# L2 attention of a four-layer net: the place of the weighing in each unit's order, and one reciprocal for two query tiles

## The chip, the cores and the metric

The kernel runs on one core of a Trainium2 chip. The metric is the device time of one execution in microseconds. Five engines work beside each other, each through its own instructions in order: TensorE (PE, its weight loads shown apart as PEld), VectorE (DVE), ScalarE (ACT), GpSimd (POOL) and SyncE (SP). They wait for each other by semaphores.

## The reference

Tokens `x` have the shape (8, 512, 128): 8 batches of 512 tokens. Four layers follow each other, each a half feed-forward, an attention and a half feed-forward. The change lies in the attention of layer 2:

```
def _L2_attn_ref(x, Wq, Wk, Wv, Wo, bo):        # 16 heads (H) of 64 (DH)
    q, k, v = x @ Wq, x @ Wk, x @ Wv            # each split into heads
    scores = einsum('bihd,bjhd->bhij', q, k) * 64**-0.5 + slope * (i - j)
    scores = where(i >= j, scores, -1e30)       # causal
    attn = softmax(scores)
    out = einsum('bhij,bjhd->bihd', attn, v)
    return out @ Wo + bo
...
x = x + 0.5 * _L1_ffn_ref(_layernorm(x), ...)   # splines chosen by two argmaxes
x = x + 0.5 * _L2_ffn_ref(_layernorm(x), ...)   # one 128x128 matrix
x = x + _L2_attn_ref(_layernorm(x), ...)
x = x + 0.5 * _L2_ffn_ref(_layernorm(x), ...)
x = x + 0.5 * _L3_ffn_ref(_layernorm(x), ...)   # 8 experts, two chosen
```

## The kernel before

`l2_block` works through 64 units. A unit is one batch and one pair of heads (`jj` 0 and 1), so eight units make a batch. The 512 queries of a unit are four tiles (`i` 0 to 3) of 128 rows; because of the causal mask tile `i` needs only 128(i+1) keys.

The work on unit n is spread over several turns of one loop, so that different units overlap. The loop runs over n from -4 to 67. Its turn n holds, in this order on TensorE:

- three groups of four transposes of unit n-1's probabilities (`turn` with m = 4, 0, 1; `tp` L1732), each copied to SBUF by ScalarE (`pt` L1734);
- the projection of q and k for unit n+1 (`pp` L1674; ScalarE copies them, `qk` L1676);
- the scores of unit n for tiles 2 and 1 (`score`, `s` L1706). VectorE adds the bias, masks and takes the minimum in one instruction for each head (`e`, `m` L1710), and ScalarE takes the exponential and at the same time its row sum into `sums` (`e` L1713);
- the last two groups of transposes of unit n-1 (m = 2, 3);
- `norm(n, 3, 0)`: VectorE turns the row sums of tile 3 into reciprocals (`rc` L1740) and multiplies both heads' probabilities with them (`e` L1743), and then the same for tile 0;
- `works(3n)`: steps of other stages that are due here;
- half of the values of a pair of units (`vp` L1687; VectorE copies them, `v` L1688), and after a batch's last unit `leave` (`op` L1766), the output projection of that batch;
- `weigh(n - 2)`: the probabilities of unit n-2 times its values, sixteen matmuls of 128x64 weights (`o` L1757), copied by ScalarE (`att` L1760);
- `norm(n, 2, 1)` on VectorE;
- `works(3n + 1)`, more steps of other stages;
- the scores of unit n+1 for tiles 3 and 0, and `works(3n + 2)`.

The other stages' steps stand in a table `todo` under due places: for each batch the layer 1 feed-forward (`sp` L1048, `pa` L1138, VectorE lines L1054 to L1155, ScalarE's Gelu L1055 and tanh L1063), the two layer 2 feed-forwards (`op` L348, L351) and the layer 3 feed-forward (`lp` L366, `lm` L416 and `lg` L417 on VectorE; `yp` L384 with four VectorE instructions each, L386), with normalising and transposing between them (POOL L219 to L275, `pt` L314, copied at L321). A batch's steps come at the same places of each batch, so most stretches of eight units look alike.

The order on TensorE, ScalarE and VectorE is that of the recording (`tc.manual_schedule`). All TensorE results but the scores go through four PSUM banks (`bank`, tag "mm", 4 buffers): a new result waits until the last result in its bank has been read. The scores have two buffers of two banks each. The framework chooses which free bank a result gets.

```
def bank(name, shape=(P, 512)):
    return ps.tile(list(shape), F32, tag="mm", name=name, bufs=4)
...
with tc.manual_schedule(engines={mybir.EngineType.PE, mybir.EngineType.Activation, mybir.EngineType.DVE}):
    for n in range(-4, last + 4):
...
def works(at):
    for work in todo.pop(at, ()):
        work()
```

Of the kernel before, what the change touches and what calls it, by code (L numbers as in the profile page):

```python
# [8 lines left out]
F32 = mybir.dt.float32  # L9
I32 = mybir.dt.int32  # L10
AF = mybir.ActivationFunctionType
ALU = mybir.AluOpType
# [4 lines left out]
P = 128  # L17
# [127 lines left out]
class Net:  # L145
# [1496 lines left out]
    def l2_block(self, w1, w2, w3, xt0):  # L1642
# [9 lines left out]

        nc, tc, a = self.nc, self.tc, self.a
        wq, wo = self.wq, self.wo
        OFF = (0, 128, 384, 768)
        with ExitStack() as c:
            pool = c.enter_context(tc.tile_pool(name="a2", bufs=1))
            wk = c.enter_context(tc.tile_pool(name="a2w", bufs=2))
            ps = c.enter_context(tc.tile_pool(name="a2p", bufs=1, space=PSUM))

            bias = pool.tile([P, 16, 512], F32, tag="bias", name="bias")

            def bank(name, shape=(P, 512)):
                return ps.tile(list(shape), F32, tag="mm", name=name, bufs=4)

            qs, ks, vs, es, mins, sums, turned, atts = {}, {}, {}, {}, {}, {}, {}, {}

            def project(n):

                b, at = n // 8, n % 8 * P  # L1670
                outs = []
                for made, m in ((qs, 0), (ks, 1)):
                    pp = bank("pp")
                    nc.tensor.matmul(pp, lhsT=wq[:, m, at : at + P], rhs=xts[b], start=True, stop=True)  # L1674
                    t = made[n] = wk.tile([P, 512], F32, tag=f"qk{m}", name="qk")
                    outs.append(lambda t=t, pp=pp, m=m: nc.scalar.activation(t, pp, AF.Copy, scale=1.0 if m else -0.125))  # L1676
                return outs

            def values(n, half):

                b, at = n // 8, n % 8 * P
                if not half:
                    vs[n] = vs[n + 1] = wk.tile([P, 4, 2 * P], F32, tag="v", name="v", bufs=2)
                vp = bank("vp", (P, 2, 2 * P))
                for i in range(2):
                    s0 = (2 * half + i) * P
                    nc.tensor.matmul(vp[:, i, :], lhsT=xts[b][:, s0 : s0 + P], rhs=wq[:, 2, at : at + 2 * P], start=True, stop=True)  # L1687
                nc.vector.tensor_copy(vs[n][:, 2 * half : 2 * half + 2, :], vp)  # L1688
# [7 lines left out]
            def score(n, i):  # L1696

                if n not in es:
                    es[n] = wk.tile([P, 2, 1280], F32, tag="e", name="e")
                    mins[n] = wk.tile([P, 2, 4], F32, tag="m", name="m")  # L1700
                    sums[n] = wk.tile([P, 2, 4], F32, tag="sm", name="sm", bufs=3)
                w = P * (i + 1)
                s = ps.tile([P, 2, 512], F32, tag="s", name="s", bufs=2)
                for jj in range(2):
                    cut = slice(64 * jj, 64 * jj + 64)
                    nc.tensor.matmul(s[:, jj, 0:w], lhsT=qs[n][cut, i * P : (i + 1) * P], rhs=ks[n][cut, 0:w], start=True, stop=True)  # L1706
                outs = []
                for jj in range(2):
                    e = es[n][:, jj, OFF[i] : OFF[i] + w]
                    nc.vector.tensor_tensor_reduce(  # L1710
                        out=e, in0=s[:, jj, 0:w], in1=bias[:, n % 8 * 2 + jj, 512 - w : 512], scale=1.0, scalar=BIG,
                        op0=ALU.add, op1=ALU.min, accum_out=mins[n][:, jj, i : i + 1])
                    outs.append(lambda e=e, jj=jj: nc.scalar.activation(  # L1713
                        e, e, AF.Exp, bias=mins[n][:, jj, i : i + 1], scale=-1.0, accum_out=sums[n][:, jj, i : i + 1]))
                return outs

            def block(n, jj, i, kt):
                lo = OFF[i] + kt * P
                return es[n][:, jj, lo : lo + P]

            def turn(n, m):


                if m == 4:
                    blocks = [(jj, i, 2) for jj in range(2) for i in (2, 3)]
                else:
                    blocks = [(m // 2, i, 1) for i in (1, 2, 3)] + [(m // 2, 3, 3)] if m % 2 else [(m // 2, i, 0) for i in range(4)]
                if n not in turned:
                    turned[n] = wk.tile([P, 5, 512], F32, tag="pt", name="pt")
                tp = bank("tp", (P, 4, P))  # L1730
                for k, (jj, i, kt) in enumerate(blocks):
                    nc.tensor.transpose(tp[:, k, :], block(n, jj, i, kt), self.ident)  # L1732
                to = turned[n][:, m, :].rearrange("p (k q) -> p k q", q=P)
                return lambda: nc.scalar.copy(to, tp)  # L1734

            def norm(n, *tiles):

                for i in tiles:
                    rc = wk.tile([P, 2], F32, tag="rc", name="rc", bufs=4)
                    nc.vector.reciprocal(rc, sums[n][:, :, i])  # L1740
                    for jj in range(2):
                        e = es[n][:, jj, OFF[i] : OFF[i] + P * (i + 1)]
                        nc.vector.tensor_scalar(e, e, rc[:, jj : jj + 1], None, ALU.mult)  # L1743

            def weigh(n):
                b, p, t = n // 8, n % 8, turned.pop(n)
                if p == 0:
                    atts[b] = wk.tile([P, 8, 512], F32, tag="att", name="att", bufs=1)
                o = bank("o")
                for kt in range(4):  # L1750
                    for jj in range(2):
                        if kt == 2:
                            src = t[:, 4, 256 * jj : 256 * jj + 256]
                        else:
                            src = t[:, 2 * jj + kt % 2, 384:512] if kt == 3 else t[:, 2 * jj + kt, 0 : 512 - kt * P]
                        lo = (n % 2) * P + 64 * jj
                        nc.tensor.matmul(  # L1757
                            o[64 * jj : 64 * jj + 64, kt * P : 512], lhsT=vs[n][:, kt, lo : lo + 64], rhs=src,
                            start=(kt == 0), stop=(kt == 3), skip_group_check=True)
                nc.scalar.copy(atts[b][:, p, :], o)  # L1760
# [17 lines left out]
            n = 3 * (last - 5)  # L1778
# [3 lines left out]
            for b in range(NB):  # L1782
                n = 3 * (8 * b - 6)
# [12 lines left out]
                n = 3 * (8 * b + 11)  # L1796
# [3 lines left out]
# [4 lines that stand above are left out]
            def run(*outs):  # L1804
                for out in outs:
                    out()

            late = []
            with tc.manual_schedule(engines={mybir.EngineType.PE, mybir.EngineType.Activation, mybir.EngineType.DVE}):
                for n in range(-4, last + 4):  # L1810
                    here, prev, two = 0 <= n < last, 1 <= n <= last, 2 <= n <= last + 1
                    if n == -1:
                        run(*project(0))
                    outs, qk, exps = [], [], []
                    if prev:
                        outs = [turn(n - 1, m) for m in (4, 0, 1)]
                    if 0 <= n and n + 1 < last:
                        qk = project(n + 1)
                    if here:
                        exps = score(n, 2) + score(n, 1)  # L1820
                    run(*outs[:2], *late[:2], *outs[2:], *late[2:], *qk, *exps[:2])
                    late = []
                    if prev:
                        run(*[turn(n - 1, m) for m in (2, 3)])
                    run(*exps[2:])
                    if here:
                        norm(n, 3, 0)
                    works(3 * n)
                    if here:
                        values(n - n % 2, n % 2)  # L1830
                    if n >= 3 and (n - 3) % 8 == 7 and n - 3 < last:
                        leave((n - 3) // 8)
                    if two:
                        weigh(n - 2)
                    if here:
                        norm(n, 2, 1)
                    works(3 * n + 1)
                    if -1 <= n and n + 1 < last:
                        late = score(n + 1, 3)
                        late += score(n + 1, 0)  # L1840
                    if -3 <= n < 5:
                        slopes(n + 3)
                    works(3 * n + 2)
                assert not todo
# [198 lines left out]
```

## Time and profile before

| what | value |
|---|---|
| median of three executions | 2611.81 us (2608.92 to 2611.95) |
| profiled execution: its own time | 2632.98 us |
| profiled execution: span from first to last instruction | 2631.2 us |
| the L2 attention's stretch (1030 to 1876 us of the span) | 846 us |
| in it TensorE busy, VectorE busy, ScalarE busy | 809.1, 666.3, 587.3 us |
| granted TensorE clock in it | 1.00 |
| VectorE reciprocals at L1740 in the whole span | 256, of 159 ns in the middle |
| time of eight units in a steady batch (1353 to 1464, for example) | 111 us |

Times in the profile are microseconds from the start of the span. A timeline row has the start, the duration, the engine, line and operation, what it writes and reads, how many instructions it merges, and in brackets how long the engine had been idle before it and who ended that wait. A matmul's end is modelled: matmuls are pipelined, and a row can start a little before the one ahead of it ends. So the cost of a group of matmuls is best read from its start to the start of the next group.

### The profile page before, as it was taken

The page shows a single profiled execution, that of the slowest core. Times are in us where ns is not written, and L with a number is a line of the kernel's source. Part 1 is how long each engine was busy: PE and PEld are TensorE (multiplying, and loading weights), DVE is VectorE, ACT ScalarE, POOL GpSimd, SP SyncE. Part 2 cuts the span into 40 slices and gives each one's busy share as a digit, 9 for nine tenths or more (in the row PEclk, how much of TensorE's full clock was granted, in tenths as well). Part 3 has the DMA queues.
Part 4 walks back from the last instruction along what each step waited for, and adds up shares of the span by engine and source line. Part 5 has one row for each costly group of instructions (what it writes and reads, how often), then busy time and mean ns, then how long its engine had stood idle before and what let it go on. Part 6 is the DMA issues. An engine that isn't in the chain of part 4 may idle for free.

```text
span 2631.2 us, 51301 instructions
## 1 busy us (share of the span) xinstructions
PE 2389.5 (91%) x18184; PEld 1427.7 (54%) x18184; DVE 2024.7 (77%) x5597; ACT 1756.3 (67%) x4393; POOL 1154.0 (44%) x2003
## 2 busy tenths in 40 slices
PE   6858756999999998999999999999899999999997
PEld 6537533344444444566565655556565666666664
DVE  5347348888888866878788787877688989898897
ACT  2135134466677666766757676676598999999984
POOL 5655643244454452163452635332234545454443
PEclk9878877799999999999999999999899999999999
DMA  8121340001010100000000000000000000000000
GB/s 270 51 81 30 93 124 1 18 18 27 19 26 19 34 2 4 1 1 1 1 1 1 1 1 1 1 1 9 9 18 9 10 22 22 10 14 22 22 2 13
DMA packets 72962, 66.51 MB, mean 25 GB/s; under 512 B 15675, under 2 KB 62787, under 8 KB 70563
## 3 DMA queue, kind: packets, MB, share of 16 engines
q1 hardware_dynamic: 68096, 54.88, 7.7%
q0 software_dynamic: 3584, 7.58, 1.0%
q8 instruction: 145, 2.38, 0.4%
q10 hardware_dynamic: 1026, 0.78, 0.1%
q14 instruction: 111, 0.90, 0.1%
HBM read 36.47 MB, written 26.80 MB: 24 GB/s over the span
## 4 chain that ended last, share of the span: by engine, by line
PE 62%; DVE 20%; ACT 9%; POOL 4%; issue 3%; DMA 1%; another core or an unknown queue 0%; SPq 0%; POOLq 0%; DVEq 0%; ACTq 0%
PE tp L1476 8%; PE s L1450 6%; PE s L1290 5%; PE o L1757 4%; PE o L1492 4%; PE o L1320 4%; PE s L1706 4%; PE yp L384 3%; ACT e L1713 3%; PE s L1310 3%; DVE nm L1291 3%; DVE nm L1454 3%; PE tp L1732 2%; PE pp L1674 2%; PE hp L684 2%
## 5 line engine op out<-in xcount | busy, mean ns | idle before, releaser
L1461 ACT ACTIVATE e<-s,nm 128x512 f32<-128x512 f32 x512 | 345.4, 689 | 26.0 <-DVE nm L1454 21.4
L1291 DVE TENSOR_REDUCE nm<-s 128x2 f32<-128x1024 f32 x256 | 301.4, 1218 | 75.9 <-PE s L1310 61.0
L1454 DVE TENSOR_REDUCE nm<-s 128x2 f32<-128x1024 f32 x256 | 301.0, 1217 | 29.6 <-PE s L1450 27.7
L1482 ACT ACTIVATE p<-tp 128x512 f32<-128x512 f32 x512 | 279.3, 618 | 61.6 <-PE tp L1476 61.6
L1312 ACT ACTIVATE pr<-s 128x512 f32<-128x512 f32 x512 | 271.6, 600 | 73.1 <-PE s L1310 69.3
L1476 PE MATMUL tp<-cst,e 128*128 128x128 f32 x2048 | 294.3, 282 | 15.2 <-DVE rs L1467 7.9
L1476 PEld LDWEIGHTS tp<-cst,e 128*128 128x128 f32 x2048 | 221.5, 142 | 153.0 <-issue 86.8
L1470 POOL TENSOR_SCALAR e<-e,rs 128x512 f32<-128x512 f32 x114 | 200.1, 1755 | 229.8 <-DVE rs L1467 191.3
L1290 PE MATMUL s<-k,q 32*128 32x512 f32 x1024 | 279.2, 657 | 18.0 <-DVE nm L1291 14.6
L1310 PE MATMUL s<-q,k 32*128 32x512 f32 x1024 | 290.4, 627 | 5.4 <-DVE at L1333 4.4
L1713 ACT ACTIVATE e<-e,m 128x512 f32<-128x512 f32 (+3 forms) x512 | 286.1, 570 | 12.6 <-DVE m L1710 12.5
L1710 DVE CUSTOM_DVE_ANT_0 e<-s,bias 128x512 f32<-128x512 f32 (+3 forms) x512 | 220.1, 485 | 92.9 <-PE s L1706 92.4
L219 POOL TENSOR_TENSOR d<-st 128x4 f32<-128x4 f32 (+3 forms) x90 | 19.7, 218 | 554.2 <-DVE st L215 356.9
L1734 ACT COPY pt<-tp 128x512 f32<-128x512 f32 x320 | 174.5, 590 | 90.1 <-PE tp L1732 90.1
L386 DVE SCALAR_TENSOR_TENSOR x<-yp,sel,x 128x128 f32<-128x128 f32 x512 | 177.9, 348 | 39.7 <-PE yp L384 26.6
L1470 DVE TENSOR_SCALAR e<-e,rs 128x512 f32<-128x512 f32 x398 | 195.5, 521 | 9.1
L1743 DVE TENSOR_SCALAR e<-e,rc 128x512 f32<-128x512 f32 (+3 forms) x512 | 190.0, 416 | 9.1
L1732 PE MATMUL tp<-cst,e 128*128 128x128 f32 x1280 | 170.9, 278 | 9.8 <-ACT pt L1734 4.0
L1450 PE MATMUL s<-k,q 32*128 32x512 f32 x1024 | 174.8, 651 | 5.1 <-ACT e L1461 2.6
L1706 PE MATMUL s<-qk 64*128 64x512 f32 (+3 forms) x1024 | 173.6, 457 | 2.0 <-DVE m L1710 1.4
L1492 PE MATMUL o<-p,va 128*32 128x128 f32 x4096 | 165.8, 277 | 2.9 <-ACT p L1482 2.9
L1732 PEld LDWEIGHTS tp<-cst,e 128*128 128x128 f32 x1280 | 139.2, 141 | 48.5 <-issue 13.3
(467 smaller groups left out, 4848.0 us busy)
## 6 DMA issues: line engine op xcount, KB each, us to landing
yd<-z SPq DMA_DIRECT2D x8, 1024.0 KB
r<-yd SPq DMA_DIRECT2D x32, 256.0 KB
sk<-pu SPq DMA_DIRECT2D x16, 256.0 KB
k<-sk SPq DMA_DIRECT2D x60, 64.0 KB
w<-in_l_w SPq DMA_DIRECT2D x14, 256.0 KB
xd<-wqkv SPq DMA_DIRECT2D x12, 256.0 KB
x<-in_x SPq DMA_DIRECT2D x8, 256.0 KB
up<-in_l_up SPq DMA_DIRECT2D x8, 256.0 KB
```

The costliest lines, as they stand in the source:

```text
L1290: nc.tensor.matmul(s[:, jj, :], lhsT=q[cut, g, i * P : (i + 1) * P], rhs=k[cut, g, :], start=True, stop=True)
L1291: nc.vector.tensor_reduce(nms[b, g // 2][:, i, 2 * h : 2 * h + 2, g % 2], s, AX.X, ALU.max, negate=True)
L1310: nc.tensor.matmul(s, lhsT=k[cut, g, kt * P : (kt + 1) * P], rhs=q[cut, g, :], start=True, stop=True)
L1450: nc.tensor.matmul(s[:, jj, :], lhsT=q[cut, g, i * P : (i + 1) * P], rhs=k[cut, g, :], start=True, stop=True)
L1454: nc.vector.tensor_reduce(nm, scores[n, h], AX.X, ALU.max, negate=True)
L1461: nc.scalar.activation(e, s[:, jj, :], AF.Exp, bias=nm[:, jj : jj + 1], accum_out=sm[:, jj : jj + 1])
L1470: (nc.gpsimd if h and jj and n >= 14 else nc.vector).tensor_scalar(e, e, rc[:, jj : jj + 1], None, ALU.mult)
L1476: nc.tensor.transpose(tp[:, kt, :], probs[n][j][:, kt * P : (kt + 1) * P], self.ident)
L1482: nc.scalar.activation(p, turns[n].pop(0), AF.Exp)
L1706: nc.tensor.matmul(s[:, jj, 0:w], lhsT=qs[n][cut, i * P : (i + 1) * P], rhs=ks[n][cut, 0:w], start=True, stop=True)
L1713: outs.append(lambda e=e, jj=jj: nc.scalar.activation(e, e, AF.Exp, bias=mins[n][:, jj, i : i + 1], scale=-1.0, accum_out=sums[n][:, jj, i ...
L1732: nc.tensor.transpose(tp[:, k, :], block(n, jj, i, kt), self.ident)
```

## The change

Three things are edited. `weigh(n - 2)` moves behind `norm(n, 2, 1)` and `works(3n + 1)`, directly ahead of the scores of unit n+1. `norm` takes one reciprocal for both tiles of its call (128x2x2 numbers) where it took one for each tile (128x2). For that the row sums' columns are put in another order, so that the tiles of a call lie beside each other (`SUM`).

```
-        OFF = (0, 128, 384, 768)
+        OFF, SUM = (0, 128, 384, 768), (1, 3, 2, 0)
...
-                        e, e, AF.Exp, bias=mins[n][:, jj, i : i + 1], scale=-1.0, accum_out=sums[n][:, jj, i : i + 1]))
+                        e, e, AF.Exp, bias=mins[n][:, jj, i : i + 1], scale=-1.0, accum_out=sums[n][:, jj, SUM[i] : SUM[i] + 1]))
...
             def norm(n, *tiles):
-                for i in tiles:
-                    rc = wk.tile([P, 2], F32, tag="rc", name="rc", bufs=4)
-                    nc.vector.reciprocal(rc, sums[n][:, :, i])
+                rc = wk.tile([P, 2, 2], F32, tag="rc", name="rc", bufs=4)
+                nc.vector.reciprocal(rc, sums[n][:, :, SUM[tiles[0]] : SUM[tiles[0]] + 2])
+                for k, i in enumerate(tiles):
                     for jj in range(2):
                         e = es[n][:, jj, OFF[i] : OFF[i] + P * (i + 1)]
-                        nc.vector.tensor_scalar(e, e, rc[:, jj : jj + 1], None, ALU.mult)
+                        nc.vector.tensor_scalar(e, e, rc[:, jj, k : k + 1], None, ALU.mult)
...
-                    if two:
-                        weigh(n - 2)
                     if here:
                         norm(n, 2, 1)
                     works(3 * n + 1)
+                    if two:
+                        weigh(n - 2)
                     if -1 <= n and n + 1 < last:
                         late = score(n + 1, 3)
                         late += score(n + 1, 0)
```

In the built program the change moves, on TensorE, the sixteen matmuls of L1757 behind the matmuls of `works(3n + 1)`, where there are any (in 50 of the 64 units); on ScalarE the copy at L1760 behind the ScalarE steps of `works(3n + 1)`. VectorE loses 128 of the 256 reciprocals and keeps its order. POOL and SyncE issue the same instructions in the same order.

## The prediction

> **What bounds the kernel now.** I read the busy sums by stage first, then TensorE's waits in the L2 stretch, then the order of TensorE around the weighing, then VectorE's and ScalarE's rows at the two places where a merged reciprocal could come late. The first row below gives window, length and then busy time of PE, PEld, DVE, ACT and POOL, granted clock, DMA.
>
> ```profile
> 1030.00:1876.00 846.00, 809.13 (x4820) 497.29 (x4816) 666.34 (x2567) 587.34 (x1629) 335.50 (x736) 1.00 0.01 2
> ```
>
> TensorE is busy for 809 of the 846 us in which the edited lines run, at the full granted clock. So it sets the pace, and about 37 us, 1.4% of the span, is all its idle time there. What ends that idle time (total, times, longest):
>
> ```profile
> PE pp L1674 <- ACT pt L1734: 8.8, 6, 2.4
> PE o L1757 <- ACT pt L1734: 7.7, 15, 1.0
> PE tp L1732 <- ACT pt L1734: 4.0, 5, 0.8
> ```
>
> These are waits for a PSUM bank, not for the weighing's data: `o` reads copies that ScalarE made a turn earlier. When another matmul stands in `o`'s place, it takes that bank and waits as long. So the 7.7 us do not go; they pass to the first matmul of `works(3n + 1)`.
>
> **The moved weighing.** TensorE in two stretches:
>
> ```profile
> 1289.31 1.03 PE L1687 MATMUL vp<-wqkv,xta 128*128 128x256 f32 x4
> 1290.27 2.37 PE L1757 MATMUL o<-pt,v 128*64 128x512 f32 x16
> 1292.57 0.66 PE L314 MATMUL pt<-cst,xn 128*128 128x128 f32 x4
> 1293.16 1.35 PE L1706 MATMUL s<-qk 64*128 64x512 f32 x8
> ```
>
> ```profile
> 1227.45 1.02 PE L384 MATMUL yp<-wall,xt 128*128 128x512 f32 x2
> 1228.31 1.03 PE L1687 MATMUL vp<-wqkv,xta 128*128 128x256 f32 x4
> 1229.27 2.37 PE L1757 MATMUL o<-pt,v 128*64 128x512 f32 x16
> 1231.57 1.12 PE L384 MATMUL yp<-wall,xt 128*128 128x512 f32 x2
> 1232.63 1.35 PE L1706 MATMUL s<-qk 64*128 64x512 f32 x8
> ```
>
> The figure before the shapes is the weight tile: `o` uses 128*64, `s` 64*128, the rest 128*128. From start to start, `yp` costs 0.86 us between two 128*128 groups and 1.06 between `o` and `s`: a change of the tile costs about 0.1 us at each side. Before: `vp` to `o` 0.96, `o` 2.30, `yp` to `s` 1.06, sum 4.32. After: `vp` to `yp` 0.86 (as `vp` before the projection L1766, 1352.12 to 1352.98), `yp` to `o` 0.96, `o` to `s` 2.30 (1313.33 to 1315.63, where no work stands between): 4.12. Saved: **0.20 us**. With the four transposes of L314: before 0.96 + 2.30 + 0.59 = 3.85; after 0.86 + 0.54 (four transposes at 0.11, and 0.10 for the change) + 2.30 = 3.70; saved **0.15 us**, which I also take for L348, of the same tiles. The built program has matmuls there in 50 units, 22 with wide ones (`yp`, `pa`, `pp`) and 28 with 128x128 ones: 22 x 0.20 + 28 x 0.15 = **8.6 us** if nothing else comes late. Matmul ends are modelled, but these are starts; still, the gain can be anything from 0 to 8.6 (no tile change is added, so a loss is excluded).
>
> [...]
>
> Everything else that moves has cover. The copy L1760 stands behind the ScalarE steps of `works(3n + 1)`; ScalarE waited for `o` there anyway, and the bank is wanted again 2.7 us later (scores 1.3, three groups of transposes 1.4). Behind Gelu (L1055, with a table load of 1.28) it still fits: the scores `sp` end 2.3 us earlier, so Gelu is done before `o` is. The tanh that follows waits for VectorE's L1061, which stands behind the score steps; those start with `s`, so ScalarE's late copies there (the 8.8 us) stay. VectorE's 17.5 us of waiting for `yp` shrink, but behind it in the order stands `s`, which is no earlier. Nothing is moved past a queue of POOL or SyncE, and no DMA moves.
>
> **The merged reciprocal.** 128 of 256 reciprocals go. One takes 0.16 us and 0.19 from start to start; no row shows one for 128x2x2 numbers, and its bounds are this row and the 0.35 of the one for 128x32 (L1088); going by numbers, two more cost 0.01. That saves 0.18 us a call (between nothing and 0.19), 23 us of VectorE, most of it idle time gained. In exchange, the products of the first tile wait for the second tile's row sum. Where ScalarE brings that sum last, the price is the first tile's two products, 0.67 us from start to start (0.75 with the last one's end). The place where it decides:
>
> ```profile
> 1302.74 0.16 DVE L1740 RECIPROCAL rc<-sm 128x2 f32<-128x2 f32 x1
> 1302.93 0.75 DVE L1743 TENSOR_SCALAR e<-e,rc 128x384 f32<-128x384 f32 x2
> 1303.92 0.17 DVE L1740 RECIPROCAL rc<-sm 128x2 f32<-128x2 f32 x1 [0.23 <-ACT e L1713]
> 1304.12 0.62 DVE L1743 TENSOR_SCALAR e<-e,rc 128x256 f32<-128x256 f32 x2
> ...
> 1307.65 0.19 DVE L417 TENSOR_TENSOR lg<-lp,lm 128x32 f32<-128x32 f32 x1
> ```
>
> From the sum at 1303.92 to the next step (1304.65) are 0.73 us; after the change 0.19 + 0.67 + 0.53 = 1.39, so VectorE is **0.66 us later**, runs without a gap to L417, and the projection takes L417's bank (it starts at 1307.98, right behind it).
>
> **A steady batch, unit by unit** (weighings at 1249, 1263, 1279, 1290, 1301, 1313, 1325, 1340; minus is earlier).
> - First to third: 0.20 + 0.15 + 0.15 saved, so TensorE is at -0.50. The waits of 0.62, 1.07, 0.80, 0.70 and 0.53 us start from TensorE's own rows and move along.
> - Fourth: VectorE is late for ScalarE there (0.68 us). Two calls save 0.38, so the exponentials and the next sums are at -0.88.
> - Fifth: the sum at -0.88, plus 0.66, puts L417 and the projection at **-0.22**. What TensorE had beyond that is lost.
> - Sixth: two calls make it -0.60 on VectorE; the waits of 0.23 (`s`) and 0.30 (L1131) shrink.
> - Seventh: the sum comes at 1326.9 - 0.60, then 1.39: L386 starts at 1327.7 where it waited for `yp` until 1328.97. But the built program now gives the projection the bank of the second `yp`, whose L386 is at 1333.80 - 1.25 = 1332.55 and ends 1.50 later: the projection starts near 1334.15 instead of 1334.27, **-0.12**.
> - Eighth: -0.20.
>
> So such a batch gives 0.3 us; five batches have this form (1131 to 1686): -1.6. The first batch (three units with work, VectorE free) gives -0.5, the seventh (TensorE busy 99.5 of 100 us, no layer 1 steps, seven units) -1.2, the last -0.7, its end -0.4. Against that, the last unit's transposes wait for L1743 (1853.10, 0.57 idle) and get their products 0.95 later, +0.95, and the second unit's +0.2 (1031.88). **Sum -3.2 us**: 2632.98 - 3.2 = 2629.8 for the profiled execution, and 2611.81 - 3.2 = **2608.6** on the median, which lies 0.8% under that execution. (Scaled by that 0.8% the sum would be the same in its first decimal.)
>
> [...]
>
> **Rivals.**
> - All is kept: VectorE's relief outweighs the wait, the 8.6 us stay and the waits of 0.15, 0.23 and 0.30 in five batches go (3.4): 2611.8 - 12.0 = 2599.8. For it: TensorE is 96% busy. Against it: L417 and the second `yp` above.
> - Slower: the reciprocal's wait. It decides wherever the second sum is the last to come and VectorE is late until TensorE next needs it. If the tile changes save nothing and it bites in the fifth and seventh unit, the projections are at +0.28 and +0.38: five batches +1.9, ends +1.15, 2614.9. If it bites in the third unit too (its sum was waited for 0.40), 0.66 x 5 more, 2618.2. For it: twelve such waits already (4.2 us). Against it: after the third unit's the VectorE row of L351 waits 1.30 for TensorE.
> - Nothing on the path: the starts of matmuls follow the array's own time, the reciprocals were covered: 2611.8.
>
> **How the numbers follow.** My forecast (2605.5 to 2610.5) gets 0.47, all kept or most of it (below 2605.5) 0.20, nothing (2610.5 to 2613) 0.15, slower by the wait 0.18. About 0.2%, 5.2 us, is what a measurement of this kernel can tell from no change: faster than 2606.6 are the second case and 0.07 of the first, 0.27; slower than 2617.0 is the upper part of the wait, 0.12; within, 0.61. The range leaves out the last few us of both rivals: 2601.5 to 2616.5; the likeliest case alone 2605.5 to 2610.5.
>
> **What would show it.** After: a group of L384 between `vp` and `o` takes 0.86 to 0.96 from start to start, and `o` to `s` 2.30; L1739 stands 128 times at 0.16 to 0.18 us; the batches from 1131 to 1686 last 110.6 us instead of 110.9, the one from 1686 (1685.78 to 1786.29 between the starts of L1766) 99.3 instead of 100.5; in the fifth unit the projection waits for L417 with TensorE idle 0.3 to 0.7, in the seventh for L386. I am wrong if the fourth unit's exponentials don't come earlier, if the idle time of TensorE grows by over 8 us (then the wait is dearer than 0.66), or if the starts of `yp` and `o` keep their old sum of 4.32.

## The result, and the profile after

The changed kernel takes 2643.36 us (median of four executions, 2640.72 to 2651.58). The kernel before took 2610.36 us beside it (2606.77 to 2611.95). The ratio is **1.0135**, with a 95% interval of 1.0123 to 1.0147: 33 us slower. The forecast was 2608.6 us, in a range of 2601.5 to 2616.5, with a chance of 0.12 for slower.

The two profiled executions can't be compared by their spans (2631.2 and 2638.9 us): that of the kernel before lost 27 us ahead of layer 2 (its first L1674 stands at 1011.31, the other's at 984.65). So I compare the stretch from the first projection L1674 to the start of the last output projection L1766, first before, then after. The columns are window, length, busy time of PE, PEld, DVE, ACT and POOL, granted clock, DMA.

```profile
1011.31:1866.85 855.54, 816.24 (x4824) 498.21 (x4825) 676.70 (x2612) 600.44 (x1667) 338.84 (x745) 1.00 0.01 3
```

```profile
984.65:1876.34 891.69, 822.45 (x4825) 503.10 (x4825) 657.04 (x2485) 598.95 (x1667) 336.40 (x745) 0.98 0.01 2
```

The whole loss is here: 36.2 us in these two executions. TensorE's idle time grew from 39.3 to 69.2 us (length less busy time), its busy time by 6.2 us, and its clock fell to 0.98. VectorE was freed of 20 us (676.7 to 657.0; 23 were forecast), and nobody needed them. A steady batch (from one start of L1766 to the next) takes 116.3 us instead of 110.9.

TensorE's waits in this stretch of the changed kernel (total, times, longest):

```profile
PE op L348 <- ACT xt L321: 23.3, 13, 2.5
PE pp L1674 <- ACT pt L1734: 9.5, 6, 2.4
PE o L1757 <- ACT pt L1734: 5.7, 13, 0.9
PE pa L1138 <- ACT k L1133: 5.3, 6, 2.3
```

Two of the four are new. The layer 2 feed-forward's matmuls L348 wait for ScalarE's copy L321 of the transposes L314, and the layer 1 matmuls L1138 for the copy L1133 of the transposes L1131: together 28.6 us, where idle time grew by 29.9 (the other waits rose and fell by up to 2.7 us and nearly cancel). Both are waits for **data**, and neither was in the kernel before. One of them in the changed kernel, TensorE and ScalarE (parts of the timeline):

```profile
1375.64 0.63 PE L314 MATMUL pt<-cst,xn 128*128 128x128 f32 x4 [0.70 <-ACT qk L1676]
1376.10 1.06 PE L1687 MATMUL vp<-wqkv,xta 128*128 128x256 f32 x4
1379.65 1.37 PE L348 MATMUL op<-we,xt 128*128 128x128 f32 x8 [2.49 <-ACT xt L321]
1380.95 3.80 PE L1757 MATMUL o<-pt,v 128*64 128x512 f32 x16
```

```profile
1377.07 1.06 ACT L1734 COPY pt<-tp 128x512 f32<-128x512 f32 x2
1378.01 0.52 ACT L1713 ACTIVATE e<-e,m 128x256 f32<-128x256 f32 x1
1378.42 0.20 ACT L1713 ACTIVATION_READ_ACCUMULATOR e<-e,m 128x1 f32 x1
1378.51 0.51 ACT L1713 ACTIVATE e<-e,m 128x256 f32<-128x256 f32 x1
1378.91 0.20 ACT L1713 ACTIVATION_READ_ACCUMULATOR e<-e,m 128x1 f32 x1
1379.00 0.59 ACT L321 ACTIVATE xt<-pt 128x512 f32<-128x512 f32 x1
```

The transposes are done at 1376.3 by the profile, but ScalarE comes to their copy only at 1379.00, behind the end of tile 2's exponentials, two copies of probabilities and the exponentials of tile 1. Before the change the weighing stood here, and TensorE did not notice. The same place in the kernel before:

```profile
1388.59 1.06 PE L1687 MATMUL vp<-wqkv,xta 128*128 128x256 f32 x4
1390.18 2.38 PE L1757 MATMUL o<-pt,v 128*64 128x512 f32 x16 [0.53 <-ACT pt L1734]
1392.49 1.16 PE L348 MATMUL op<-we,xt 128*128 128x128 f32 x8
```

```profile
1391.50 0.59 ACT L321 ACTIVATE xt<-pt 128x512 f32<-128x512 f32 x1
```

The copy ends at 1392.09, 0.4 us before L348 starts. Take the weighing out, and L348 could start at 1389.65 (behind `vp`), but its operand still comes at 1392.1: a wait of 2.5 us where `o` had one of 0.53, readable from these rows before anything was run.

The second thing to see in the changed kernel is that `o`, behind that wait, takes 3.80 us instead of 2.37. Windows of 3.4 us around it:

```profile
1377.00:1380.40 3.40, 0.91 (x7) 0.75 (x7) 2.12 (x8) 2.81 (x10) 2.69 (x10) 1.00 0.00 0
1380.40:1383.80 3.40, 3.40 (x12) 1.33 (x12) 2.40 (x7) 0.00 (x0) 3.04 (x8) 0.51 0.00 0
1383.80:1387.20 3.40, 3.40 (x29) 2.35 (x26) 1.35 (x5) 1.14 (x3) 1.98 (x2) 0.99 0.00 0
```

The column behind POOL is the granted clock: for 3.4 us after the wait TensorE runs at half speed, which costs 1.7 us. The trace's clock record has eight such stretches in this part of the changed kernel, one in the kernel before: seven more, 12 us.

So a steady batch adds up: L348's two waits 2.49 and 0.83, L1138's 0.60, a wait of the projection for a bank that grew from 1.07 to 1.50, the low clock 1.7, together 6.0; measured 5.3. The other 0.7 us come from work saved: TensorE's busy time in a batch grew by only 0.9 us (105.50 to 106.36), of which the low clock alone would make 1.7. The other waits come to nearly nothing together.

### The profile page after: what moved, and what is told of

Its sections match the earlier page's. It is cut to its first block, busy times and chain, and to the rows that moved or that the text cites. A ratio compares the mean times of both kernels' runs of the same rounds, so it can differ in the third digit from the quotient of the medians.

```text
span 2638.9 us, 51145 instructions
## 1 busy us (share of the span) xinstructions
PE 2385.6 (90%) x18184; PEld 1427.2 (54%) x18184; DVE 2003.9 (76%) x5469; ACT 1753.6 (66%) x4393; POOL 1149.7 (44%) x2003
## 4 chain that ended last, share of the span: by engine, by line
PE 58%; DVE 22%; ACT 12%; POOL 4%; issue 2%; DMA 1%; SPq 0%; POOLq 0%; DVEq 0%; ACTq 0%
PE tp L1476 8%; PE s L1450 6%; PE s L1290 5%; ACT e L1713 5%; PE o L1492 4%; PE o L1320 4%; PE o L1757 4%; DVE nm L1291 3%; PE s L1310 3%; PE s L1706 3%; PE yp L384 3%; DVE nm L1454 3%; ACT pt L1734 2%; DVE e L1710 2%; PE tp L1732 2%
## 5 line engine op out<-in xcount | busy, mean ns | idle before, releaser
L1476 PEld LDWEIGHTS tp<-cst,e 128*128 128x128 f32 x2048 | 221.7, 142 | 152.6 <-issue 86.8
L1734 ACT COPY pt<-tp 128x512 f32<-128x512 f32 x320 | 173.8, 590 | 68.7 <-PE tp L1732 68.7
L386 DVE SCALAR_TENSOR_TENSOR x<-yp,sel,x 128x128 f32<-128x128 f32 x512 | 177.8, 348 | 26.4 <-PE yp L384 13.5
L1743 DVE TENSOR_SCALAR e<-e,rc 128x512 f32<-128x512 f32 (+3 forms) x512 | 176.8, 411 | 4.5
L1757 PE MATMUL o<-pt,v 128*64 128x512 f32 (+3 forms) x1024 | 162.3, 462 | 5.7 <-ACT pt L1734 5.7
```

What stands on the lines that cost most here:

```text
L1476: nc.tensor.transpose(tp[:, kt, :], probs[n][j][:, kt * P : (kt + 1) * P], self.ident)
```

## The experiments

**Theory A**: the weighing was the cover for ScalarE's copies between the transposes of `works(3n)` and the matmuls that read them in `works(3n + 1)`; that happens in three turns of eight (`n % 8` of 3 and 4 for L348, 0 for L1138). The low clock is a consequence of the waits. **Rival R**: the merged reciprocal's wait, my own slower rival. **Rival C**: the new place is dear in every turn (later copy L1760, longer-held bank).

The kernel before took 2642 to 2644 us in its runs beside these experiments, so their ratios count, not their times, and lengths of stretches in the traces. In all ten traces, as in that of the kernel before, the first L1674 stands at 1011 to 1025 us, where the changed kernel's stands at 985: in the traces most of the longer time lies ahead of layer 2. Its cause is open. The diffs are against the changed kernel where nothing else is said.

**1. The move alone.** Against the kernel before:

```
-                    if two:
-                        weigh(n - 2)
                     if here:
                         norm(n, 2, 1)
                     works(3 * n + 1)
+                    if two:
+                        weigh(n - 2)
```

> The weighing is moved as in the change, the reciprocals stay two to a call. Theory A (lost cover: the weighing's 2.3 us of matmuls stood between the transposes L314 or L1131 and the matmuls L348 or L1138 that read their copies, and hid ScalarE's copies L321 and L1133): the whole loss is here, 2640 to 2647 us against 2643.4 of the full change, with about 23 us of waits of L348 for L321 and 5 us of L1138 for L1133. Theory R (the price is the wait of a tile's products for the other tile's row sum in the merged reciprocal, as my slower rival had it): the loss is gone, 2606 to 2613 us.

Measured: ratio 1.0131 (1.0110 to 1.0152). The waits are those of the full change:

```profile
PE op L348 <- ACT xt L321: 23.3, 13, 2.5
PE pp L1674 <- ACT pt L1734: 10.6, 6, 2.4
PE pa L1138 <- ACT k L1133: 5.3, 6, 2.3
```

The whole loss is the move's. (Its time of 2678.5 us lies outside the 2640 to 2647 that I wrote down, because the kernel before took 32 us more beside it than beside the change; the ratio is what was expected.)

**2. The merged reciprocals alone.**

```
+                    if two:
+                        weigh(n - 2)
                     if here:
                         norm(n, 2, 1)
                     works(3 * n + 1)
-                    if two:
-                        weigh(n - 2)
```

> The reciprocals are merged as in the change, the weighing stays at its old place. Theory A: 2607 to 2614 us, within 0.2% of the kernel before, and TensorE never waits for L321 by L348. Theory R: 2635 to 2645 us.

Measured: ratio 0.9993 (0.9979 to 1.0008); its 2640.59 us stand beside 2642.16 of the kernel before, so they don't speak for R, whose times were written for 2610. R falls. The new wait that my prediction saw for the fifth unit is there, though, in each of the five steady batches, in this kernel's waits:

```profile
PE o L1757 <- ACT pt L1734: 6.7, 14, 0.5
...
PE pp L1674 <- DVE lg L417: 3.4, 5, 0.7
```

Forecast as 0.66 us of delay on VectorE, it shows as 0.69 of idle TensorE, and the steady batch is 111.1 us instead of 110.9.

**3. The cover kept in three turns.**

```
+                    if two and n % 8 in (0, 3, 4):
+                        weigh(n - 2)
                     if here:
                         norm(n, 2, 1)
                     works(3 * n + 1)
-                    if two:
+                    if two and n % 8 not in (0, 3, 4):
                         weigh(n - 2)
```

> The whole change, but in three turns of eight (n % 8 of 0, 3 and 4), where a step of works(3n + 1) reads what ScalarE copies after works(3n), the weighing keeps its old place. Theory A: the waits of L348 for L321 and of L1138 for L1133 are gone (under 1 us each), the granted clock is 1.00 again in the steady batches, and the time is 2603 to 2611 us: the kernel before, less the tile changes in the units that stay moved. Theory R: the merged reciprocals are all still there, over 2630 us. Theory C (the move costs the same in every unit, because the copy L1760 comes later and holds a PSUM bank longer): five eighths of the loss stay, about 2630 us.

Measured: ratio 0.9979 (0.9963 to 0.9996), 2640.15 us beside 2642.16. Both data waits are gone, with five eighths of the moves still made; C falls too. What stands at the top of this kernel's waits now:

```profile
PE o L1757 <- ACT pt L1734: 12.4, 27, 0.9
PE pp L1674 <- ACT pt L1734: 8.8, 6, 2.4
PE tp L1732 <- DVE e L1743: 4.8, 3, 1.6
```

Here the saved tile changes can be followed. The stretch from the first L1674 to the last L1766 in experiment 2's kernel and in this one (same reciprocals), whose low-clock stretches are alike:

```profile
1019.88:1880.20 860.32, 818.77 (x4824) 500.07 (x4825) 659.66 (x2484) 599.43 (x1667) 336.31 (x745) 0.99 0.01 3
```

```profile
1024.82:1883.80 858.98, 814.75 (x4825) 500.84 (x4826) 661.38 (x2485) 599.68 (x1667) 337.23 (x745) 0.99 0.01 3
```

TensorE's busy time falls by 4.0 us, and `o`'s waits for a bank rise by 5.7 (6.7 to 12.4). TensorE gets through its work sooner and waits more for ScalarE's copies L1734. The steady batch ends at 110.77 us, 0.16 below the kernel before.

**4. Work put into the wait.**

```
             op = bank("op", (P, 4, P))
+            for i in range(fill):
+                nc.tensor.matmul(op[:, i % 4, :], lhsT=self.ident, rhs=w["w"], start=True, stop=True)
             for i in range(4):
                 nc.tensor.matmul(op[:, i, :], lhsT=xt[:, i * P : (i + 1) * P], rhs=w["w"], start=True, stop=True)
...
                 n = 3 * (8 * b + 11)
-                self.plan(todo, (n, n + 3, n + 4), *self.l2_ffn_steps(b, w2, bank))
+                self.plan(todo, (n, n + 3, n + 4), *self.l2_ffn_steps(b, w2, bank, fill=8))
```

> The whole change, and ahead of the matmuls L348 of the second layer 2 feed-forward of a batch eight more matmuls of 128x128 by 128 columns on operands that are long there (weights of the layer, the identity), into the same PSUM tile, which the real ones then overwrite. They add about 2 us of work to a wait of 2.3 to 2.5 us. If the low granted clock after that wait (0.61 and 0.54 in two windows of 2 us, the weighing of 3.80 instead of 2.37 us) comes from the idle time, it stays at 1.00: the weighing behind it takes 2.37 us again, and the time falls by 7 to 10 us, to 2633 to 2637. If the idle time has nothing to do with it, the time stays at 2642 to 2646 us.

Measured: ratio 1.0085 (1.0063 to 1.0107), 0.0046 or some 12 us less than the move alone beside it; in the traces the stretch is 9.3 us shorter than that of the full change. (The times that I wrote down were again for the kernel before at 2610 us.) The place in this kernel's timeline, where the lines behind L348 stand two higher, and the granted clock in its two windows:

```profile
1399.44 1.06 PE L1689 MATMUL vp<-wqkv,xta 128*128 128x256 f32 x4
1401.04 2.05 PE L348 MATMUL op<-we,cst 128*128 128x128 f32 x16 [0.54 <-ACT pt L1736]
1403.00 1.16 PE L350 MATMUL op<-we,xt 128*128 128x128 f32 x8
1404.09 2.37 PE L1759 MATMUL o<-pt,v 128*64 128x512 f32 x16
```

```profile
1401.04:1403.00 1.96, 1.96 (x17) 1.86 (x17) 0.68 (x3) 1.96 (x7) 1.72 (x8) 1.00 0.04 8
1403.00:1406.40 3.40, 3.40 (x27) 2.03 (x26) 2.67 (x10) 0.16 (x1) 2.96 (x8) 1.00 0.00 0
```

L348's operand comes no earlier, but the weighing behind it takes 2.37 us again. Useless matmuls made the kernel faster than idling did: the low clock comes from the idle time, and in a steady batch it is worth 1.5 us (114.72 against 116.27).

**5. The reader one place later.**

```
-                    self.plan(todo, (n, n + 3, n + 4), *self.l2_ffn_steps(b, w2, bank))
+                    self.plan(todo, (n, n + 3, n + 5), *self.l2_ffn_steps(b, w2, bank))
```

The same edit stands at both feed-forwards.

> The whole change, and the matmuls L348 of both layer 2 feed-forwards stand one due place later, behind the weighing and the next scores (3.6 us of matmuls), so that the moved weighing is their cover again. Theory A (lost cover): the waits of L348 for L321 go, and with them the low clock; what stays is L1138's wait for L1133 (5.3 us and its clock) and, in the turns where L1048 reads a copy of L321 too, a part of the 0.8 us of each. Ratio to the kernel before 1.000 to 1.006, where the full change has 1.0135. If the weighing's new place is dear for another reason (its copy L1760 or its bank), the ratio stays over 1.010.

Measured: ratio 1.0046 (1.0029 to 1.0064). L348 waits no more, but L1048, which follows it in one of the turns and reads a copy of L321 itself, is now the first to stand there, and waits longer than the part of 0.8 us that I gave it:

```profile
PE o L1757 <- ACT pt L1734: 8.5, 21, 0.9
PE sp L1048 <- ACT q L321: 6.9, 6, 1.3
PE pp L1674 <- ACT pt L1734: 5.8, 6, 1.6
PE pa L1138 <- ACT k L1133: 5.3, 6, 2.3
```

**6. The copy earlier on ScalarE.**

```
-                    run(*exps[2:])
                     if here:
                         norm(n, 3, 0)
                     works(3 * n)
+                    run(*exps[2:])
```

> The whole change, and on ScalarE the two exponentials of tile 1 (with the reading of their sums about 1.0 us) stand behind the ScalarE steps of works(3n) instead of ahead of them. Theory A says that the wait is ScalarE's queue ahead of the copy: L348's waits shrink by about 1.0 us each, from 23.3 to 10 to 12 us in total, L1138's of 5.3 to under 2, the longest waits fall under 1.6 us and the low clock goes with them: ratio 1.003 to 1.008, if the later exponentials cost nothing. If the wait is set by something else than that queue (the transposes' own latency, the bank), the waits keep their length and the ratio is 1.012 to 1.016.

Measured: ratio 1.0011 (0.9993 to 1.0029), a little better than expected. L348's waits shrink as forecast, L1138's from 5.3 to 1.3, and the low clock is nearly gone (one stretch of 3.4 us is left):

```profile
PE op L348 <- ACT xt L321: 11.4, 8, 1.5
PE pp L1674 <- ACT pt L1734: 7.8, 6, 2.4
```

So the length of the wait is ScalarE's queue ahead of the copy: 1.0 us of exponentials out of its way shortened the longest wait from 2.49 to 1.52.

**7. The cover kept, two reciprocals.** Against the kernel before, whose `norm` and columns of sums stay:

```
-                    if two:
+                    if two and n % 8 in (0, 3, 4):
                         weigh(n - 2)
                     if here:
                         norm(n, 2, 1)
                     works(3 * n + 1)
+                    if two and n % 8 not in (0, 3, 4):
+                        weigh(n - 2)
```

> The weighing moved except in the three turns of eight where it is the cover, and two reciprocals to a call as before. It tells what of the 0.9979 of the same move with merged reciprocals belongs to which part. If the move in the other turns brings it: ratio 0.996 to 0.999 and steady batches of 110.6 to 110.8 us. If the merging brought it: 0.999 to 1.001 and 110.9 us.

Measured: ratio 0.9990 (0.9971 to 1.0008), steady batches of 110.8 us. By the batches the move in the other turns brings the 0.1 to 0.2 us; the ratio, whose interval takes in both cases, doesn't tell.

**8. The cover kept in one turn.** Against experiment 3:

```
-                    if two and n % 8 in (0, 3, 4):
+                    if two and n % 8 == 4:
...
-                    if two and n % 8 not in (0, 3, 4):
+                    if two and n % 8 != 4:
```

> The whole change, but the weighing keeps its old place in one turn of eight (n % 8 of 4), the one in which L348 waited 2.3 to 2.5 us. Theory A: seven waits of 16.8 us in total and the low clock behind five of them (about 1.6 us each) go, and the rest of the loss stays (six waits of the other L348 and six of L1138): 33 - 17 - 8, so 6 to 11 us above the kernel before, ratio 1.002 to 1.005, steady batches of 112 to 112.6 us. If the loss lies in all moved turns alike, seven eighths stay: ratio 1.011 to 1.013.

Measured: ratio 1.0041 (1.0020 to 1.0062). One turn of eight holds some two thirds of the loss. The others' waits are left as they were:

```profile
PE op L348 <- ACT xt L321: 6.3, 6, 2.2
PE pa L1138 <- ACT k L1133: 5.3, 6, 2.3
```

The steady batch of 113.0 us is 0.4 longer than the upper end that I gave: I had not counted the projection's longer wait for its bank, 1.53 us here and 1.07 again in experiment 3, where the second unit's weighing stays too. That part of the loss comes with the move in that unit's turn; by what way was not followed.

**9. The cover kept, and the copy earlier.** Against experiment 3, the edit of experiment 6:

```
-                    run(*exps[2:])
                     if here:
                         norm(n, 3, 0)
                     works(3 * n)
+                    run(*exps[2:])
```

> The whole change with the weighing kept in the three turns where it is the cover, and the exponentials of tile 1 behind the ScalarE steps of works(3n). Theory A: with the weighing as cover no copy L321 or L1133 is late, so an earlier copy has nothing to give: ratio within 0.002 of the same kernel without it (0.9979 in the earlier call, 0.996 to 1.000). If the late exponentials cost something of their own (they hold up the second reciprocal of a turn), it shows here as 1.000 to 1.003.

Measured: ratio 0.9993 (0.9978 to 1.0007), steady batches of 111.1 us against 110.8 in experiment 3. Where the weighing covers, the earlier copy gives nothing, and the later exponentials cost 0.3 us a batch.

**10. Experiment 3 once more**, with no edit.

> The whole change with the weighing kept in the three turns, once more: its interval reached from 0.9963 to 0.9996, its sister with two reciprocals gave 0.999 (0.9971 to 1.0008), and both show steady batches of 110.8 us against 110.9. If the trace's 0.2 us a batch is all, the ratio is 0.998 to 1.000.

Measured: ratio 0.9994 (0.9978 to 1.0010). Together with the first 0.9979 this is no gain that I would build on: the change, with its loss taken out, is worth 0.16 us in a batch of 110.9. No version here beats the kernel before by more than a measurement tells.

## Why the prediction was wrong

- **The step that failed** is "Everything else that moves has cover." Under it I followed what the weighing itself needs and triggers (its copy L1760, its bank, Gelu, VectorE), and never asked what the weighing had been covering where it stood. L348 and L1138 read copies that ScalarE starts in the same turn, and the 2.3 us of matmuls in between were the time for it. Experiments 1, 3, 5, 6 and 8 show this from five sides. The rows of before gave the price: 2.5 us at the longest, where the sum had nothing.
- **"These are waits for a PSUM bank, not for the weighing's data"** was true of `o` by the rows and the wrong question for its successor. "It takes that bank and waits as long" holds for `yp` (its wait of 0.53 stands at 1427.38 in the changed kernel), but L348 and L1138 waited for their own data, which no wait in the kernel before announced, because it had been hidden.
- **The third unit** of my walk through the batch (weighing at 1279), where I counted 0.15 us saved, is the turn of the 2.49 us wait; the second is that of the 0.83, the seventh that of L1138's. "TensorE is at -0.50" behind these three was the wrong term. Of the waits that were to "move along", the 1.07 grew to 1.50.
- **The clock** was no term of the sum. I took 1.00 from the profile as given; with waits of 2.3 to 2.5 us it was not. Seven stretches at 1.7 us make about 12 us. With the 29.9 us of idle time that is more than the 36 lost, because some 6 us of TensorE's work were saved (its busy time grew by only 6.2).
- **The tile changes** were there as work, but priced too high in some turns and kept as time too generously. Behind the output projection the way from L1766 to `s` fell from 10.64 to 10.44 us, as forecast. From `vp` over `yp` and `o` to `s` it fell from 4.32 to 4.24 in the five steady batches (4.16 in experiment 3), not to 4.12. In the two turns of a batch with L314 alone `o` now waits 0.27 and 0.58 us for a bank, and the way from `vp` to `s` is 4.04 and 4.45 us instead of 3.85 and 3.95 (experiment 3): there nothing was gained. The steady batch was to gain 0.3 us; with the cover kept, and five of eight turns moved, it gained 0.16.
- **The merged reciprocal** was right: 128 of them, 0.173 us in the middle, VectorE freed of 20 us that it did not need, a delay of 0.66 us where the second sum comes last (0.69 measured in experiment 2), and next to nothing on the end (0.9993). In the changed kernel that wait for L417 is only 0.18 us, below the 0.3 to 0.7 that I named, and the projection's wait for L386 in the seventh unit is not there.
- **The slower rival** rested on that reciprocal alone, so its price ended at 2618.2 us and its chance was small. One of the signs that I named for being wrong, TensorE's idle time growing by over 8 us, did come (29.9), but the reading that I tied to it, a dearer wait of the reciprocal, is false.

## What to carry to other kernels

Before moving work on the engine that sets the pace, list for each instruction behind the old place when its operands land: what is late there without the moved work is the price, and it can be read from the trace of before by pulling the block out of the rows. A wait that doesn't exist in a profile may be one that is hidden exactly by the block that you want to move. And work that is saved on the pacing engine is time only until its next wait for another engine: in experiment 3, 4.0 us less of it came with 5.7 us more of `o`'s waits.

## What the runs showed of the hardware

A wait of TensorE of about 2 us can cost more than its length: behind the one of 2.49 us at 1379.65, `o` took 3.80 us instead of 2.37. In the changed kernel the granted clock fell to one half for 3.4 us just behind the five waits of 2.48 or 2.49, and behind single ones of 2.39, 2.27 and 2.26; it did not behind another of 2.27, one of 2.15, or the waits of 1.50. In the kernel before the one such stretch stands behind a wait of 2.12 (1161.11). The wait of 2.39 or 2.40 us ahead of the second unit's projection was followed by half clock in the changed kernel (1034.81) and not in the kernel before (1060.63).

What tells these apart is where the wait falls. The clock record changes only at steps of 3.413 us (in the traces of before and after every change lies within 0.005 us of that grid), and the busy time of TensorE in one step goes with the clock of the next. The changed kernel's two waits of 2.27 us, each with the step around it and the next:

```profile
1721.78:1725.19 3.41, 1.54 (x10) 1.17 (x12) 3.08 (x12) 1.81 (x6) 2.29 (x9) 1.00 0.00 0
1725.19:1728.60 3.41, 3.41 (x16) 1.47 (x12) 0.42 (x1) 0.00 (x0) 2.97 (x8) 0.50 0.00 0
1824.17:1827.59 3.42, 1.67 (x12) 1.27 (x14) 2.94 (x10) 1.70 (x6) 0.00 (x0) 1.00 0.02 5
1827.59:1831.00 3.41, 3.41 (x28) 1.86 (x25) 0.80 (x2) 0.58 (x1) 0.00 (x0) 1.00 0.00 0
```

In the traces of before and after, from the first L1674 to the last L1766, the steps at full clock ahead of the nine stretches at half clock have TensorE busy for 0.92 to 1.54 us, the other 491 for 1.67 or more. Over all twelve traces, each from its first L1674 to its last L1766, 31 of the 33 steps at full clock that half clock follows have TensorE busy for 1.63 us or less, and all but two of the other 2963 for 1.65 or more (the exceptions: 1.85 in experiment 5 and 2.05 in experiment 6 with low clock behind them, 1.52 in experiment 6 and 1.54 in experiment 7 without). So by these runs the border lies a little under half of a step, and a wait of 2.1 to 2.5 us crosses it or not by its place. Part of the 12 us is therefore chance: a steady batch of the changed kernel takes 116.27 us, nearly 34 steps (116.05), so its waits of 2.49 us fall nearly alike, all on the dear side. In experiment 1, where the batches have other lengths (115.3 to 118.3 us), the last of the five waits of 2.49 us (at 1656.15) has no low clock behind it.
